# Two graph-attention layers in fp32: work moved at the edges of every stage, fillers for TensorE in two gaps, and the last attention's scaling on GpSimd

## The chip, the core and the metric

The kernel runs on one core of one Trainium2 chip. It uses five engines that run side by side, each with an instruction queue of its own: TensorE (PE in the profile) for matrix products, VectorE (DVE), ScalarE (ACT), GpSimd (POOL) and SyncE (SP), which here only starts transfers. The metric is the time of one execution on the device in microseconds (us); lower is better. Everything is in fp32.

## The reference, cut to what matters

There are N = 4096 nodes with F = 512 features, four heads of D = 128 features, and an adjacency matrix `adj` of 0 and 1. Both layers are residual and normalise their input first:

```python
# layer 0
h   = relu(layernorm(x));  Xw = per head: Xh @ W
s   = sigmoid(f1[:, None] + f2[None, :])          # f1, f2: one number a node and head
att = softmax of adj*s over the neighbours        # both masks are adj, so one attention
Xn  = batchnorm(att @ Xw)                         # the encoder's attention
emb = batchnorm(elu(Xn @ We.T + be) + Xn)         # MLP block
Y   = elu((att @ emb) @ W.T)                      # the decoder's attention, same weights
x   = x + batchnorm(elu(Y @ Wd.T + bd) + Y)       # MLP block
# layer 1
h     = relu(layernorm(x));  feats = h @ W1[head]
logit = leaky_relu(e_s[:, None] + e_n[None, :], 0.2), masked by adj
x     = x + relu(softmax(logit) @ feats + b)      # the last attention ("gat")
```

## The kernel before

**Stages.** The kernel runs through: a front (layer norm of row groups of 512 nodes, transposition, head values and scores), the encoder's attention `enc`, an MLP block, products with W, the decoder's attention `dec`, a second MLP block with residual, layer 1's layer norm and values, and the last attention `gat`. Features mostly lie along the 128 partitions and nodes along the free axis.

**An attention** (`attention()`, L212 to L427) is a loop over 8 blocks (4 heads times 2 halves of TB = 2048 target nodes). Each block has 32 steps j, one per 128 source nodes. A step makes one tile of unnormalised weights `e` of 128x2048. For `enc` and `dec` it is tanh and exp on ScalarE and a product with the mask on VectorE (L435 to L437); for `gat` a relu on ScalarE (L833) and one VectorE instruction that adds a column and multiplies by the mask (L834). TensorE then multiplies the values of the 128 sources with the tile into four PSUM banks of 128x512 (L359; the fourth bank joins at step EVICT = 2, and takes the first two steps then, L356). `weight_tile` (L239 to L244) hands out the buffers for `e`: two come from the pool `keep`, which outlives the MLP blocks, the others from a pool of the attention itself. As `made` is counted up before it is tested, the first tile comes from the own pool and the next ones follow in turn; of each cycle of EP + ebufs tiles, two are from `keep`.

**The softmax's denominators** are sums of the weight tiles over all sources. For each block three lists at L62 to L68 say how a step is summed: "moved" steps are added into a buffer by an accumulating transfer that GpSimd issues (L373), "by ones" steps are summed on TensorE by four matmuls with ones (L252), and all others are added to `acc` on VectorE (L379, L381). At a block's end PE sums the buffers with ones too; with the flag True in `GAT`, the moved buffer's sum follows in the next block's step 1. The decoder reads every fifth weight tile back from memory (`ekeep`, L333) and uses the inverses of the encoder.

**A block's end** is spread over the next block's steps (`ending`, L284 to L301): outputs leave PSUM on ScalarE (`out_gat` L839), denominators are inverted, spread over the partitions by small transfers that GpSimd issues (L277), and each of the four 128x512 outputs is multiplied by its inverse (`scaled_gat`, L843, on VectorE) and goes through a relu with bias (L846) to an accumulating transfer into the output (L852). The last block has no block after it: after its last weight it takes the denominators, then the last step's products (`early` at L363), inverts on VectorE, spreads the inverses by a matmul (L425) and adds the residual on VectorE (L849).

**MLP block and layer 1.** `mlp_block` multiplies 128x512 tiles on PE (L592), takes elu as exp and relu on ScalarE (L612, L613) and two VectorE instructions, and collects the batch norm's statistics. Sixteen small matmuls sum the decoder's MLP weights for its bias (L682), issued where the decoder's attention begins. After the second MLP block, 16 small matmuls build score columns (L726), copied into `w1x` at L728; `residual` (L692 to L706) applies the batch norm and adds x, and `centred` (L733 to L754) takes, for each of eight groups of 512 nodes, the mean by a matmul with 1/F over a sum `S`, three or four differences, relu and squares on ScalarE, and a reduction over the four feature groups (L753). `deviation` (L756) makes the standard deviations, L776 the values and scores of each 128 nodes, L781 their copies. GpSimd sums the values (L787). Then the maximum of the scores is found and broadcast (L796 to L805), exponentials of scores are taken (L807 to L815), and `gat` starts with `row0`, the first row of target scores, which was stored and loaded back (L791 to L793).

**What sets the order.** A scheduler places the instructions of each engine by its own estimates, subject to the data and to edges written by hand: `tc.issue_after(i)` and `pinned([...])` put instructions behind i in their engine's queue. Within a queue the order is then fixed: an instruction that waits holds back all behind it.

Of the kernel before, what the change touches and what calls it, by code (L numbers as in the profile page):

```python
# [31 lines left out]
FP = mybir.dt.float32  # L32
# [8 lines left out]
IB = 512  # L41
# [25 lines left out]
GAT = tuple(range(3, 28, 2)), (30, 31), True  # L67
GAT_LAST = (3, 5, 7, 9, 11, 13, 15, 17, 19, 21, 23), (12, 30, 31)  # L68
# [16 lines left out]
def kernel(ctx, tc, x, xT, adjT, w0, w0T, v0, wencT, wdecT, vecs, w1, w1T, a1, outT):  # L85
# [21 lines left out]
    def bank1():  # L107
        return psum1.tile([P, IB], FP, name="den")

# [102 lines left out]
    def attention(what, keep, pools, weights, values, row_of, out, finish, ebufs, modes=None, invert=None,  # L212
                  kept=None, sums=None, sums2=None, extras={}, row0=None, masks0=()):
# [25 lines left out]
        def weight_tile():  # L239
            nonlocal made  # L240
            made += 1
            if made % (EP + ebufs) < EP:
                return keep.tile([P, TB], FP, name="e", tag="ek", bufs=EP)
            return spool.tile([P, TB], FP, name="e", bufs=ebufs)  # L244
# [66 lines left out]
        for n, (h, tb) in enumerate(blocks):  # L311
# [6 lines left out]
            po, ahead = [bank() for _ in range(SB - 1)], []  # L318
            adds, held, stores, next_row = [], [], [], None
            for j in range(NJ):  # L320
# [4 lines left out]
                with pinned([a_load, *products_of] if j else []):  # L325
                    if (n, j) in extras:
                        extras[n, j](a_load)
                    if not last and j == NJ - 10:
                        next_row = next_row_of(*blocks[n + 1])
# [4 lines left out]
                else:  # L334
# [5 lines left out]
                    products_of = weights(e, rowb, a, j, h, SB if n + j == 0 else 1)  # L340
# [23 lines left out]
                early = last and j == NJ - 1 and invert is not None  # L364
                if not early:
                    products()
# [28 lines left out]
                if early:  # L395
                    products()
# [5 lines left out]
            if not last:  # L402
# [6 lines left out]
                continue  # L409
            outs = [out(spool, h, tb, s, po[s]) for s in range(SB)]  # L410
# [31 lines left out]
    with tc.tile_pool(name="keep", bufs=1) as keep:  # L442

        with tc.tile_pool(name="f_small", bufs=1) as small, tc.tile_pool(name="f_work", bufs=2) as work:
# [26 lines left out]
            for ib in range(NIB):  # L471
                st = work.tile([P, C, 6], FP, name="st")
                mv = work.tile([P, C, 2], FP, name="mv")

                with pinned([first_hn] if ib == 1 else []):
                    for c in range(C):
                        nc.vector.bn_stats(st[:, c, :], xs[ib][:, c, :])
                for c in range(C):
                    nc.vector.bn_aggr(mv[:, c, :], st[:, c, :])
                rstd = work.tile([P, C], FP, name="rstd")  # L480
                last_dve = rsqrt(rstd, mv[:, :, 1], LN_EPS)
                hT = work.tile([P, C, IB], FP, name="hT")
                for c in range(C):
                    by_pool = c == C - 1
# [99 lines left out]
        def mlp_block(work, w, src, dst, gamma, beta, scale, between, early=None):  # L584
# [5 lines left out]
            def product(z, o, ib, lo, hi):  # L590
                for fb in range(lo, hi):
                    nc.tensor.matmul(z, w[:, fb, o * P:(o + 1) * P], nodes(src[fb], ib),  # L592
                                     start=(fb == 0), stop=(fb == C - 1))

            for o in range(C):
# [7 lines left out]
                for ib in range(NIB):  # L603
# [3 lines left out]
                    else:  # L607
                        z = bank()
                        product(z, o, ib, 0, C)
# [12 lines left out]
                last = bn_coefs(stats, gamma, beta, a_mlp, b_mlp, o, o + 1)  # L622
            return last
# [42 lines left out]

        nc.sync.dma_start(w, wdecT.rearrange("(c p) o -> p c o", p=P))
        with tc.tile_pool(name="dec", bufs=1) as spool:
            attention("dec", keep, spool, tanh_weights, xc, lambda h, tb: (rows[tb], h), out_dec, (scaled, elu), 4,
                      kept="read")  # L670
# [5 lines left out]
    with tc.tile_pool(name="l_small", bufs=1) as small, tc.tile_pool(name="l_work", bufs=2) as work:  # L676
        x1 = [R[2]] + [small.tile([P, N], FP, name=f"x1_{o}") for o in range(1, C)]

        pb = bank1()
        for o in range(C):  # L680
            for fb in range(C):
                nc.tensor.matmul(pb[:, o:o + 1], w[:, fb, o * P:(o + 1) * P], ones[:, 0:1],  # L682
                                 start=(fb == 0), stop=(fb == C - 1))
        nc.vector.tensor_sub(bias, vec_of("dec_mlp_b"), pb[:, 0:C])
# [7 lines left out]
        def residual(o, ib):  # L692
# [4 lines left out]
            nc.vector.tensor_add(d, d, xt)  # L697
            if o == 1:
                nc.gpsimd.tensor_add(S[ib], nodes(x1[0], ib), d)
            elif o > 1:  # L700
# [4 lines left out]
            elif ib == NIB - 1:  # L705
                nc.sync.dma_start(outT[o * P:(o + 1) * P, :], x1[o])  # L706

# [7 lines left out]
        last_coefs = mlp_block(work, w, xd, x1, "dec_mlp_bn_gamma", "dec_mlp_bn_beta", None,  # L715
# [6 lines left out]
        pw = bank1()  # L722
        for fb in range(C):
            for h in range(H):
                k = 2 * (fb * H + h)
                nc.tensor.matmul(pw[:, k:k + 2], w1Ts[:, h, fb * P:(fb + 1) * P], a1s[:, h, :], start=True, stop=True)  # L726
        with tc.issue_after(last_coefs.ins):
            nc.vector.tensor_copy(w1x[:, :, :, D:DX], pw[:, 0:2 * C * H].rearrange("p (c h s) -> p c h s", h=H, s=2))  # L728
# [4 lines left out]
        def centred(ib):  # L733
# [3 lines left out]
            residual(C - 1, ib)  # L737
            pm = bank()
            nc.tensor.matmul(pm, mean_of, S[ib], start=True, stop=True)
# [6 lines left out]
            for fb in range(C):  # L746
                if ib:
                    nc.scalar.activation(sq[:, fb, :], d[:, fb, :], AF.Square)
                nc.scalar.activation(hT[:, fb, :], d[:, fb, :], AF.Relu)  # L749
# [3 lines left out]
            nc.vector.tensor_reduce(S[ib], sq.rearrange("p c n -> p n c"), AX.X, ALU.add)  # L753
            return hT  # L754
# [9 lines left out]
        hT = centred(0)  # L764
        rstd = deviation(0)
        for ib in range(NIB):
            for c in range(C):

                if c == 1 and ib < NIB - 1:
                    hT_next = centred(ib + 1)  # L770
                j = ib * C + c
                r = rstd[:, c:c + 1]
                for k in range(2):
                    b = bank()
                    for fb in range(C):
                        nc.tensor.matmul(b[:, 0:2 * DX], hT[:, fb, c * P:(c + 1) * P],  # L776
                                         w1x[:, fb, 2 * k:2 * k + 2, :].rearrange("p h x -> p (h x)"),
                                         start=(fb == 0), stop=(fb == C - 1))
                    pv = heads_of(b)
                    for h in range(2):  # L780
                        nc.scalar.activation(block(v1[2 * k + h], j), pv[:, h, 0:D], AF.Identity, scale=r)  # L781
                    nc.vector.tensor_scalar_mul(scores_of(j, k), pv[:, :, D:DX], r)
# [7 lines left out]
            if ib == SB - 1:  # L790
                store_rows(rows1[0], targets(0))  # L791
                row0 = w.rearrange("p c f -> p (c f)")
                load_row(row0, rows1[0], 0)  # L793
# [4 lines left out]
        nc.tensor.transpose(pt[0:H, 0:P], mloc, ident)  # L798
# [5 lines left out]
        nc.tensor.matmul(pm[:, 0:H], ones[0:H, :], mdiag, start=True, stop=True)  # L804
# [4 lines left out]
        last_act = nc.scalar.activation(jcol, jcol, AF.Exp)  # L809
        nc.vector.tensor_scalar_mul(nq, jcol2, -1.0)  # L810

        for row, in in_parts(SB, row0):
            last_dve = nc.vector.tensor_scalar(row, row, mbc[:, 0:1], G_MAX, ALU.add, ALU.min)
            with tc.issue_after(last_act.ins):
                last_act = nc.scalar.activation(row, row, AF.Exp, scale=0.8)  # L815

    def rest_of_rows(load):

        pss = bank()
        for h in range(H):  # L820
            nc.tensor.matmul(pss[:, h:h + 1], vacc[:, h, :], ones[:, 0:1], start=True, stop=True)
# [9 lines left out]
    def gat_weights(e, rowb, a, j, h, parts):  # L831
        for e, rowb, a in in_parts(parts, e, rowb, a):
            last_act = nc.scalar.activation(e, rowb, AF.Relu, bias=column(nq, j, h), scale=column(jcol, j, h))  # L833
# [8 lines left out]
    def scaled_gat(spool, h, tb, s, o, rb, last):  # L842
        nc.vector.tensor_mul(o, o, rb)  # L843
# [10 lines left out]
    with tc.tile_pool(name="gat", bufs=1) as spool:  # L854
        x1_last = []

        def load_last(load):
# [3 lines left out]
        attention("gat", spool, spool, gat_weights, v1, lambda h, tb: (rowsg, tb * H + h), out_gat,  # L861
                  (scaled_gat, add_to_output), 7, lambda n: (GAT_FIRST, *[GAT] * (H * NTB - 2), GAT_LAST)[n],
# [44 lines left out]
```

## Time and profile before

| what | value |
|---|---|
| time, median of 3 runs (range) | 3273.88 us (3273.81 to 3275.61) |
| span of the profiled execution | 3271.8 us |
| busy PE / DVE / ACT / POOL | 3196.2 / 2675.9 / 2600.1 / 465.7 us |
| products of weights and values, L359 | 2628.8 us over 6048 records |
| gat's weights, L834 (128x2048 form) | 593.0 us, mean 2332 ns |
| gat's additions to the sum, L381 (R<-R,e) | 278.0 us over 121, mean 2298 ns |

The profile's page gives busy time by engine, by line and by a chain that ended last. A group's row names line, engine, operation, output and inputs, count, busy time, the mean of one instruction in ns, and the engine's idle time before them with what ended it. A fp32 matmul shows as two records, and its weight load (PEld) overlaps other matmuls. PE's clock is what the chip granted, 1.0 being full speed; it is read per stretch of time, as busy time alone does not tell a slow matmul from a fast one.

### The profile page before, as it was taken

To read this page: it belongs to the slowest core of one execution; us is meant where nothing else is said; L and a number is where in the kernel's file an instruction comes from. 1 tells how busy PE (TensorE), PEld (TensorE's weight loads), DVE (VectorE), ACT (ScalarE), POOL (GpSimd) and SP (SyncE) were. 2 spreads that over 40 slices of the span, in tenths; PEclk is the share of its full clock that TensorE was granted. 3 is DMA by queue.
4 is the path that set the end of the run, shared out by engine and by line. 5 is a ranking of instruction groups with operands and counts; after the bars stand their busy time and mean duration, and the time that the engine had idled before them with its cause. 6 is when DMAs were issued, how large, how long until landed. Compare 5 with 4: busy or idle time off the path is not lost.

```text
span 3271.8 us, 26021 instructions
## 1 busy us (share of the span) xinstructions
PE 3196.2 (98%) x8719; PEld 1484.0 (45%) x8719; DVE 2675.9 (82%) x1916; ACT 2600.1 (79%) x1901; POOL 465.7 (14%) x622
## 2 busy tenths in 40 slices
PE   7999999999999999999999999999999999999999
PEld 6334434444444464444444444448644444444443
DVE  6999999999999665656665665586599999999997
ACT  7999999999997449999999999565666666665663
POOL 3001211211210000000000000024312222222221
PEclk9999999999999999999999999999999999999999
DMA  9998988988986023444443444232398999889985
GB/s 208 196 195 228 268 222 225 266 222 230 271 234 157 0 68 126 151 130 136 140 151 127 132 148 133 63 132 79 84 213 214 219 228 244 214 204 236 224 217 135
DMA packets 211151, 578.48 MB, mean 177 GB/s; under 512 B 25069, under 2 KB 28173, under 8 KB 195017
## 3 DMA queue, kind: packets, MB, share of 16 engines
q0 software_dynamic: 67968, 222.51, 35.9%
q1 hardware_dynamic: 126432, 293.72, 27.1%
q10 hardware_dynamic: 16616, 60.60, 4.7%
q8 instruction: 68, 1.11, 0.1%
q14 instruction: 67, 0.54, 0.0%
HBM read 377.10 MB, written 84.29 MB: 141 GB/s over the span
## 4 chain that ended last, share of the span: by engine, by line
PE 73%; DVE 10%; ACT 7%; issue 5%; DMA 5%; POOL 0%; DVEq 0%; ACTq 0%; SPq 0%; POOLq 0%
PE ps L359 58%; PE ps L592 7%; DVE e L437 6%; ACT e L435 4%; PE ps L776 3%; DMA a<-mask 3%; ACT e L436 2%; DVE acc L381 2%; DMA acc<-e 2%; PE den L252 1%; PE ps L356 1%; PE ps L648 1%; PE ps L516 1%; DMA rinvs<-dcol 1%; PE ps L498 0%
## 5 line engine op out<-in xcount | busy, mean ns | idle before, releaser
L359 PE MATMUL ps<-e,R 128*128 128x512 f32 x6048 | 2628.8, 595 | 40.3 <-DVE e L437 32.9
L359 PEld LDWEIGHTS ps<-e,R 128*128 128x128 f32 x6048 | 1147.0, 191 | 1512.8 <-issue 1420.0
L437 DVE TENSOR_TENSOR e<-e,a 128x2048 f32<-128x2048 f32 (+1 forms) x470 | 1052.4, 2261 | 381.3 <-ACT e L436 367.1
L435 ACT ACTIVATE e<-rowb,score 128x2048 f32<-128x2048 f32 (+1 forms) x470 | 912.7, 1968 | 102.1 <-PE ps L359 58.1
L436 ACT ACTIVATE e<-e 128x2048 f32<-128x2048 f32 (+1 forms) x470 | 871.0, 1880 | 6.4
L833 ACT ACTIVATE e<-rowb,nq,jcol 128x2048 f32<-128x2048 f32 x224 | 460.8, 2089 | 269.2 <-DMA w<-e 136.6
L834 DVE SCALAR_TENSOR_TENSOR e<-e,jcol,a 128x2048 f32<-128x2048 f32 (+1 forms) x259 | 593.0, 2332 | 10.8 <-ACT e L833 10.8
L381 DVE TENSOR_TENSOR acc<-acc,e 128x2048 f32<-128x2048 f32 x130 | 297.3, 2287 | 2.1
L381 DVE TENSOR_TENSOR R<-R,e 128x2048 f32<-128x2048 f32 x121 | 278.0, 2298 | 0.0
L373 POOL DMA_DIRECT2D w<-e x178 | 150.3, 847 | 609.4 <-DMA w<-e 383.3
L592 PE MATMUL ps<-R,w 128*128 128x512 f32 x512 | 220.3, 592 | 0.6 <-DVE w L550 0.6
L373 POOL DMA_DIRECT2D acc<-e x144 | 120.4, 880 | 540.8 <-DMA acc<-e 222.9
L277 POOL DMA_DIRECT2D rb<-rinvs x60 | 34.2, 574 | 1062.5 <-DVE R L540 871.6
L592 PEld LDWEIGHTS ps<-R,w 128*128 128x128 f32 x512 | 97.2, 190 | 122.7 <-issue 117.4
L776 PE MATMUL ps<-w1x,hT 128*128 128x260 f32 x512 | 118.5, 391 | 1.8 <-ACT hT L749 1.8
L612 ACT ACTIVATE ex<-ps,bias 128x512 f32<-128x512 f32 x64 | 44.0, 687 | 95.9 <-PE ps L592 78.8
L776 PEld LDWEIGHTS ps<-w1x,hT 128*128 128x128 f32 x512 | 98.7, 194 | 21.6 <-ACT hT L749 3.4
L833 ACT ACTIVATE e<-w,nq,jcol 128x2048 f32<-128x2048 f32 (+1 forms) x35 | 65.7, 1938 | 30.8 <-DMA R<-e 30.8
L614 DVE SCALAR_TENSOR_TENSOR ex<-ex,re 128x512 f32<-128x512 f32 x64 | 45.0, 704 | 36.1 <-ACT re L613 35.9
L781 ACT ACTIVATE R<-ps,rstd 128x128 f32<-128x128 f32 x128 | 38.3, 369 | 38.1 <-PE ps L776 37.0
L787 POOL TENSOR_TENSOR vacc<-vacc,R 128x128 f32<-128x128 f32 x120 | 53.0, 468 | 57.5 <-ACT R L781 57.5
L252 PE MATMUL den<-e,ones 128*32 128x512 f32 x440 | 53.0, 598 | 0.0
(162 smaller groups left out, 1228.6 us busy)
## 6 DMA issues: line engine op xcount, KB each, us to landing
a<-mask SPq DMA_DIRECT2D x720, 256.0 KB, 4.3
w<-e POOLq DMA_DIRECT2D x178, 512.0 KB, 6.6
acc<-e POOLq DMA_DIRECT2D x144, 512.0 KB, 7.0
ekeep<-e ACTq DMA_DIRECT2D x48, 1024.0 KB, 7.4
e<-ekeep SPq DMA_DIRECT2D x48, 1024.0 KB, 4.9
mask<-in_adjT POOLq DMA_DIRECT2D x8, 2048.0 KB, 104.5
rowb<-rows SPq DMA_DIRECT2D x16, 1024.0 KB, 8.0
rb<-rinvs POOLq DMA_DIRECT2D x60, 256.0 KB, 4.5
```

Of the source, the lines that this page charges most:

```text
L252: last_ones = nc.tensor.matmul(den[s * 32:(s + 1) * 32, :], ones[:, 0:32], t[:, s * IB:(s + 1) * IB], start=start, stop=stop)
L359: last_main = nc.tensor.matmul(b, block(values[h], j), e[:, s * IB:(s + 1) * IB], start=(j == 0), stop=(j == NJ - 1))
L373: nc.gpsimd.dma_start(into_half, e_half, **({"accum_op": ALU.add} if j > moved[0] else {}))
L381: nc.vector.tensor_add(acc, acc, e)
L435: nc.scalar.activation(e, rowb, AF.Tanh, bias=column(score[:, 1], j, h), scale=0.5)
L436: last_act = nc.scalar.activation(e, e, AF.Exp, scale=0.5)
L437: last_dve = nc.vector.tensor_mul(e, e, a)
L592: nc.tensor.matmul(z, w[:, fb, o * P:(o + 1) * P], nodes(src[fb], ib), start=(fb == 0), stop=(fb == C - 1))
L776: nc.tensor.matmul(b[:, 0:2 * DX], hT[:, fb, c * P:(c + 1) * P], w1x[:, fb, 2 * k:2 * k + 2, :].rearrange("p h x -> p (h x)"), start=(fb = ...
L787: nc.gpsimd.tensor_add(vacc[:, h, :], vacc[:, h, :], block(v1[h], j))
L833: last_act = nc.scalar.activation(e, rowb, AF.Relu, bias=column(nq, j, h), scale=column(jcol, j, h))
L834: last_dve = nc.vector.scalar_tensor_tensor(e, e, column(jcol2, j, h), a, ALU.add, ALU.mult)
```

## The change

It edits the transitions between stages and the last attention:

- *Front:* in the first row group, mean and deviation of the first 128 rows are computed by themselves, ahead of the other three.
- *Decoder's start:* the count in `weight_tile` starts one earlier, so the first two weight tiles of each attention come from `keep` and can be made while the stage before still holds its memory. The 16 sums of MLP weights move into steps 6 and 16 of the decoder's second block. The first eight weights of the decoder are kept in order on ScalarE.
- *Layer 1's start:* fillers (`stay_busy`, matmuls of constants into unused banks) stand among the 16 small matmuls; the first group's mean is taken by two matmuls so that the last feature group needs no addition before it; the copy to `w1x` is put after the first residual; the first two groups of values are multiplied ahead of the first deviation; the reduction becomes two additions.
- *Last attention's start:* fillers between the maximum's transpose, broadcast and four small matmuls; `row0`'s exponentials are taken quarter by quarter among the first weights, of which three steps are made in quarters; `row0` is stored and loaded one group of nodes later.
- *Last attention:* the multiplication by the inverses goes to GpSimd except in the last block; step 30 is summed on VectorE, no longer by ones (in the last block neither 30 nor 31 is); in the last block the products of the last two steps come after the denominators, bank by bank.

The fillers compute nothing that is used: they are there so that PE's clock is not lowered. The purpose of the rest is to have work ready for PE at the edges of the stages, and to take additions off PE and multiplications off VectorE. The core of the diff:

```diff
-GAT = tuple(range(3, 28, 2)), (30, 31), True
-GAT_LAST = (3, 5, 7, 9, 11, 13, 15, 17, 19, 21, 23), (12, 30, 31)
+GAT = tuple(range(3, 28, 2)), (31,), True
+GAT_LAST = (3, 5, 7, 9, 11, 13, 15, 17, 19, 21, 23), (12,)
...
+    def stay_busy(behind, n=1, cols=IB):
+        for _ in range(n):
+            with tc.issue_after(behind.ins):
+                behind = nc.tensor.matmul(bank()[:, 0:cols], ident, w0Ts.rearrange("p h d -> p (h d)")[:, 0:cols],
+                                          start=True, stop=True)
+        return behind
...
-            if made % (EP + ebufs) < EP:
+            if (made - 1) % (EP + ebufs) < EP:
...
-                with pinned([a_load, *products_of] if j else []):
+                with pinned([a_load, *products_of, last_main] if j else []):
...
-                    products_of = weights(e, rowb, a, j, h, SB if n + j == 0 else 1)
+                    with pinned(products_of[:1] if kept == "read" and n == 0 and j < 8 else []):
+                        products_of = weights(e, rowb, a, j, h, SB if NJ * n + j < in_parts0 else 1)
...
-                early = last and j == NJ - 1 and invert is not None
-                if not early:
+                if last and invert is not None and j >= NJ - (1 if kept is not None else 2):
+                    late.append((j, e))
+                else:
                     products()
...
+            for s, b in enumerate(po):
+                for k, t in late:
+                    nc.tensor.matmul(b, block(values[h], k), t[:, s * IB:(s + 1) * IB], start=(k == 0),
+                                     stop=(k == NJ - 1))
...
+                last_dve = deviations(0, 1 if ib == 0 else C)
...
+                    if ib == 0 and c == 1:
+                        last_dve = deviations(1, C)
...
-                      kept="read")
+                      kept="read", extras={(1, 6): sums_of_weights, (1, 16): bias_of_decoder})
...
         for fb in range(C):
-            for h in range(H):
-                k = 2 * (fb * H + h)
-                nc.tensor.matmul(pw[:, k:k + 2], w1Ts[:, h, fb * P:(fb + 1) * P], a1s[:, h, :], start=True, stop=True)
+            with tc.issue_after(last_pe.ins):
+                for h in range(H):
+                    k = 2 * (fb * H + h)
+                    last_pe = nc.tensor.matmul(pw[:, k:k + 2], w1Ts[:, h, fb * P:(fb + 1) * P], a1s[:, h, :],
+                                               start=True, stop=True)
+            last_pe = stay_busy(last_pe)
...
+            if ib == 0:
+                with tc.issue_after(last_pe.ins):
+                    nc.tensor.matmul(pm, mean_of, S[ib], start=True, stop=False)
+                nc.tensor.matmul(pm, mean_of, nodes(x1[C - 1], ib), start=False, stop=True)
+                with tc.issue_after(added.ins):
+                    nc.vector.tensor_copy(w1x[:, :, :, D:DX],
+                                          pw[:, 0:2 * C * H].rearrange("p (c h s) -> p c h s", h=H, s=2))
+            else:
+                nc.tensor.matmul(pm, mean_of, S[ib], start=True, stop=True)
...
-            nc.vector.tensor_reduce(S[ib], sq.rearrange("p c n -> p n c"), AX.X, ALU.add)
+            nc.vector.tensor_add(sq[:, 0:2, :], sq[:, 0:2, :], sq[:, 2:4, :])
+            nc.vector.tensor_add(S[ib], sq[:, 0, :], sq[:, 1, :])
...
+        hT, last_relu = centred(0)
+        ahead = [values(hT, c) for c in range(2)]
+        with tc.issue_after(ahead[-1][1].ins):
+            rstd = deviation(0)
...
+    last_pe = stay_busy(last_pe, 3)
...
     def gat_weights(e, rowb, a, j, h, parts):
+        last_act = last_exp
         for e, rowb, a in in_parts(parts, e, rowb, a):
+            if row_parts:
+                row = row_parts.pop(0)
+                with tc.issue_after(last_act.ins), tc.issue_after(last_scalars.ins):
+                    if len(row_parts) < SB - 1:
+                        held(row)
+                    nc.scalar.activation(row, row, AF.Exp, scale=0.8)
...
     def scaled_gat(spool, h, tb, s, o, rb, last):
-        nc.vector.tensor_mul(o, o, rb)
+        (nc.vector if last else nc.gpsimd).tensor_mul(o, o, rb)
```

## The prediction

> **What bounds the kernel now.** I read the page first (engine shares, the chain that ended last), then busy time by stretches, then the chain and the timeline where stretches show idle time.
>
> ```profile
> PE 3196.2 (98%) x8719; PEld 1484.0 (45%) x8719; DVE 2675.9 (82%) x1916; ACT 2600.1 (79%) x1901; POOL 465.7 (14%) x622
> PE 73%; DVE 10%; ACT 7%; issue 5%; DMA 5%; POOL 0%; DVEq 0%; ACTq 0%; SPq 0%; POOLq 0%
> ```
>
> TensorE works 98% of the span, so only its gaps, its slow stretches and its own work can give anything. The stretches (columns: PE, PEld, DVE, ACT, POOL, clock, DMA share, GB/s):
>
> ```profile
> 2193.00:2205.00 12.00, 6.08 (x36) 4.21 (x34) 9.48 (x20) 9.06 (x14) 0.00 (x0) 0.68 0.27 87
> 2205.00:2212.00 7.00, 6.98 (x17) 5.43 (x18) 6.51 (x7) 3.60 (x7) 0.00 (x0) 0.57 0.44 151
> 2337.00:2345.00 8.00, 1.09 (x6) 0.51 (x4) 4.24 (x13) 6.40 (x12) 0.87 (x3) 0.74 0.51 164
> 2345.00:2352.00 7.00, 7.00 (x17) 3.67 (x18) 5.03 (x9) 7.00 (x6) 1.08 (x2) 0.57 0.62 200
> 2925.49:3039.46 113.97, 113.97 (x290) 49.31 (x289) 110.27 (x55) 71.47 (x42) 25.57 (x30) 1.00 0.92 219
> ```
>
> Each gap (before layer 1's values, before the last attention) is followed by about 7 us at clock 0.57. The last line is one block of the last attention: PE sets its 113.97 us, but VectorE needs 110.27 of it. The chain at the decoder's start:
>
> ```profile
> 1194.79 2.58 PE ps L359 x6
> 1197.37 0.86 PE ps L356 x2
> 1198.22 4.24 PE den L682 x32
> ...
> 1202.57 2.30 DVE e L437
> ...
> 1205.01 5.46 PE ps L359 x6
> 1210.46 1.17 PE ps L356 x2
> 1211.63 3.43 PE ps L359 x8
> ```
>
> Two records are one matmul: a 128x512 one takes 3.43/4 = 0.86 us, and 1.8 after a gap (5.46/3).
>
> **What the Trainium skill says.** "TensorE: Matmul & The Clock Gate", section "Part 1: The HAM clock gate", says an idle window of about 3.4 us halves the clock until PE has been busy about as long; the trace agrees (gaps of 2.5 to 5 us, then 0.57), though here recovery takes up to 7 us. "SBUF — State Buffer", section "Who interferes with whom", says a VectorE instruction with two SBUF inputs contends with a GpSimd one that reads SBUF, and the later one blocks. The timeline shows it:
>
> ```profile
> 2185.78 1.58 POOL L701 TENSOR_TENSOR S<-S,x 128x512 f32<-128x512 f32 x1 [2.01 <-DVE x L697]
> 2186.27 1.64 DVE L617 TENSOR_TENSOR x<-R,ex 128x512 f32<-128x512 f32 x1
> 2189.26 0.69 DVE L617 TENSOR_TENSOR x<-R,ex 128x512 f32<-128x512 f32 x1
> ```
>
> The same addition takes 0.69 us alone and 1.64 beside a GpSimd addition: 0.95 lost. The same section says that tensor_reduce never contends; no run here shows that.
>
> **The change, part by part.**
>
> *Front.* One row group's mean and deviation go first. They need about 1.6 us after the data at 4.07 (0.69 + 0.18, then root and reciprocal), so the first transpose moves from 9.5 to about 6.5; but the fourth group, normalised on GpSimd (2.35 us), starts 0.6 later. The encoder behind is held by ScalarE (tanh and exp take about 3.7 us a step, PE 3.43) and by mask transfers. I take 0, bounds +1 and -1.
>
> *Decoder's start.* j=1's weights come from the pool that outlives the MLP, so they are made before it; the 16 small matmuls (4.24 us) move to block 1. From 1194.6 PE does j=0 and j=1, 8 x 0.86 = 6.9, to 1201.5. j=2: ScalarE from 1194.8, tanh and exp 3.9, VectorE 2.3, ready at 1201.1; j=3 is ready 3.7 later, PE wants it 3.4 later; j=4 is loaded. So j=2 starts at 1201.5, not 1211.5: -10.0. PE never waits in this attention afterwards, so the small matmuls cost 4.2 there. Net -5.8 (-4 to -6.5).
>
> *Layer 1's start.* Now, from the MLP's last product (2193.4) to the last value product (2337.4), 144.0. After: 16 small matmuls 3.6 and four fillers 3.4 end at 2200.5; two mean matmuls end at 2202.2 (the sum over the last feature group is no longer awaited); VectorE's first difference 0.7, ScalarE's first relu 0.6 (it no longer stands behind eight residuals, 5.75 us): first product at 2203.6, warm. The two prepared groups end at 2211.6, deviation 1.0, next mean 0.9, two groups 7.1: 2220.6. The second block's square sums arrive there too. Then six periods of 15.78 (measured steady), 0.15 for a transpose, last deviation and 32 products 15.1: 2330.5. That is -6.8 (-3.5 to -7.5). The reduction (3.77 us) becomes additions of about 1.2 and 0.7; in the steady part this is hidden by PE.
>
> *Last attention's start.* The maximum, shift and exponentials shrink by about 0.7 us; fillers (0.4, 0.4, 2.6) keep PE warm. Twelve quarter steps take ScalarE 0.70 each. PE reaches j=2 14.6 us after the last value product, not 18.5. But VectorE reaches j=4 only 0.9 earlier, since its work is unchanged, and at the first block's end it adds every step (2.26 + 2.20 = 4.47 us a step against 3.43). Now its lead at j=31 is only 0.35 us (weight ready at 2455.36, PE starts it at 2455.7). So only -1.2 survives (-3.5 if VectorE were faster).
>
> *Blocks 1 to 6.* PE loses one ones-step: 0.9, to 113.08. VectorE's demand, from one block's last weight to the next one's while it never waits, is 110.2 (32 x 2.26 + 16 x 2.20 + 4 x 0.60 + 0.25). The added step gives +2.2, the four scalings leave (-2.4): 110.0. But four GpSimd multiplications of 128x512 read SBUF among saturated two-input VectorE work. GpSimd's cost per block is 4 x 1.26 and lies in its waits; VectorE's stall is bounded by 0 and 1.07 each, and I take the 0.96 seen most: 3.8. So 113.85: VectorE sets the pace, 6 x (113.85 - 113.92) = -0.4. Behind a waiting multiplication on GpSimd stand the accumulating transfers (its queue waits 21 us a block for the sum buffer, so there is room), and the relu on ScalarE waits for it (37 us idle a block).
>
> *Tail.* The last block has 19 additions (17 before): VectorE needs 32 x 2.26 + 19 x 2.20 + 0.25 + 3.8 = 118.3 from PE's j=31 of block 6. PE reaches the denominators at 3.4 + 1.8 + 30 x 3.43 + 1.8 = 110.0 and idles 8.3, so it is cold: denominator and eight late products 7.8 + 3.0, then the 9.8 from the broadcasts to the end: 138.9. Before: 3271.8 - 3139.2 = 132.6. So +6.3 (-5 if VectorE kept a lead).
>
> Sum: -5.8 - 6.8 - 1.2 - 0.4 + 6.3 = -7.9, 3273.9 to 3266.0.
>
> **Rivals.** (a) *GpSimd stalls VectorE little.* For: the mask is an 8-bit operand, and no such pair is in the trace. Against: the pair above. Then PE paces: blocks 6 x -0.9 = -5.4, VectorE's lead returns, and the tail is 110.0 + 0.9 + 6.9 + 9.8 = 127.6, -5.0: -24.2, 3250. (b) *The starts give about half* (a late weight or transfer takes a gap's place; the decoder's j=3 has 0.25 us to spare): -6.9 - 0.4 + 6.3 = -1.0, 3273. (c) *Slower:* each of 28 multiplications holds VectorE for its stretched 1.65 us, queued relus and transfers adding to it: 28 x 0.69 = 19 more, 3285. Against it: the room on GpSimd and ScalarE.
>
> **Numbers.** Main case 0.55, (a) 0.22, (b) 0.13, (c) 0.10. The main case has about 3 us either way, its edge being 3267.3 for 0.2%: faster 0.60, same 0.29, slower 0.11. The range takes in (a) and (b): 3249 to 3275.
>
> **What would show it.** Right: the second and third gap without clock below 0.9; j=2 of the decoder about 7 us after its first product; 137 us between MLP and last value product; VectorE without idle time in blocks 1 to 6 and periods near 113.9; additions and weights beside the multiplications stretched to 3.2 us; PE idle some 8 us before the last denominators. Periods of 113.1 with VectorE waiting would mean (a); PE waits at the starts (b); periods over 115 (c).

## The result, and the profile after

The changed kernel takes 3280.55 us (median of 20 runs, 3273.35 to 3287.45) against 3276.04 us (20 runs) for the kernel before: ratio 1.0014, interval 1.0008 to 1.0021. It is slightly slower, by about 4.5 us; 3266 us, faster, had been predicted. Engine shares and the chain that ended last, on the page of the changed kernel:

```profile
PE 3201.0 (98%) x8675; PEld 1482.5 (45%) x8675; DVE 2695.5 (82%) x1911; ACT 2594.5 (79%) x1908; POOL 550.8 (17%) x650
...
PE 51%; DVE 22%; issue 12%; ACT 8%; DMA 5%; POOL 0%; DVEq 0%; ACTq 0%; POOLq 0%
```

Busy shares hardly moved. The chain did: PE's part fell from 73% to 51% and VectorE's rose from 10% to 22%, so in part of the kernel VectorE now sets the end. The next view is busy time by stretches of the changed kernel (PE, PEld, DVE, ACT, POOL, clock, DMA share, GB/s): the start of layer 1, the start of the last attention, one of its blocks, and the wait before the last denominators with the stretch behind it.

```profile
2196.00:2206.00 10.00, 8.56 (x42) 5.34 (x42) 6.43 (x16) 4.09 (x7) 0.00 (x0) 1.00 0.17 52
2206.00:2213.00 7.00, 7.00 (x32) 5.95 (x33) 4.03 (x6) 4.36 (x8) 0.00 (x0) 1.00 0.09 34
...
2336.00:2340.00 4.00, 4.00 (x7) 1.67 (x6) 2.77 (x5) 3.94 (x7) 0.00 (x0) 0.58 0.54 191
2909.91:3024.85 114.94, 113.91 (x284) 48.79 (x280) 114.87 (x52) 68.01 (x40) 36.53 (x34) 1.00 0.94 220
3249.00:3258.00 9.00, 0.43 (x4) 0.00 (x0) 8.97 (x5) 0.00 (x0) 0.00 (x0) 0.78 0.00 0
3258.00:3265.00 7.00, 6.81 (x15) 2.39 (x16) 4.18 (x3) 0.69 (x1) 0.00 (x0) 0.55 0.00 0
```

In the traces the clock is 1.0 or 0.5 and nothing between; 0.57 or 0.73 is a mean over the stretch. Layer 1 starts at full clock now (0.68 and 0.57 before). The last attention's start still has half clock for a while (0.58 in 2336 to 2340). In the block VectorE is busy 114.87 us of 114.94, and PE has idle time, which it had not in this stage before. At the end PE stands still for nearly 9 us and then works at half clock for most of 7.

Where the time went, stage by stage, worked out from the starts of instructions in the traces. The second trace of the old stages is that of experiment 4, which is the kernel before up to the last attention:

| stretch | before (second trace) | after | change | predicted |
|---|---|---|---|---|
| start to the decoder's first product | 1194.6 (1198.0) | 1199.8 | not clear | 0 |
| decoder's attention | 888.9 (886.6) | 886.0 | -1.6 (mean of 9 traces 886.1) | -5.8 |
| MLP's last product to last value product | 143.8 (142.3) | 136.4 | -6.7 | -6.8 |
| last value product to first denominators | 121.6 (121.5) | 120.9 | -0.6 | -1.2 |
| blocks 1 to 6 of the last attention | 683.5 (683.5) | 686.8 | +3.3 | -0.4 |
| last block to the end | 129.4 (129.5) | 139.1 | +9.6 | +6.3 |

The last five rows add to +4.0, which is the measured difference within its interval; the second MLP block, 109.4 us in both, is left out. The first row scatters by itself: over the twelve traces of kernels with changed starts it runs from 1197.3 to 1205.3, so no single trace tells anything of a few us there.

### The profile page after: what moved, and what is told of

It reads as the page before. It is cut to its first block, busy times and chain, and to the rows that moved or that the text cites. A ratio compares the mean times of both kernels' runs of the same rounds, so it can differ in the third digit from the quotient of the medians.

```text
span 3278.9 us, 26053 instructions
## 1 busy us (share of the span) xinstructions
PE 3201.0 (98%) x8675; PEld 1482.5 (45%) x8675; DVE 2695.5 (82%) x1911; ACT 2594.5 (79%) x1908; POOL 550.8 (17%) x650
## 4 chain that ended last, share of the span: by engine, by line
PE 51%; DVE 22%; issue 12%; ACT 8%; DMA 5%; POOL 0%; DVEq 0%; ACTq 0%; POOLq 0%
PE ps L371 37%; PE ps L613 7%; DVE e L452 7%; DVE e L904 6%; DVE R L394 6%; ACT e L450 4%; PE ps L809 3%; DMA a<-mask 3%; DVE acc L394 2%; ACT e L451 2%; DMA acc<-e 2%; PE ps L670 1%; DMA rinvs<-dcol 1%; ACT e L903 1%; PE ps L537 1%
## 5 line engine op out<-in xcount | busy, mean ns | idle before, releaser
L904 DVE SCALAR_TENSOR_TENSOR e<-e,jcol,a 128x2048 f32<-128x2048 f32 (+1 forms) x265 | 620.9, 2378 | 2.8 <-ACT e L903 2.8
L394 DVE TENSOR_TENSOR R<-R,e 128x2048 f32<-128x2048 f32 x129 | 297.2, 2304 | 0.3
L913 POOL TENSOR_TENSOR R<-R,rb 128x512 f32<-128x512 f32 x28 | 80.1, 2865 | 27.0 <-DMA rb<-rinvs 27.0
L846 POOL TENSOR_TENSOR vacc<-vacc,R 128x128 f32<-128x128 f32 x120 | 65.9, 580 | 45.2 <-ACT R L839 44.8
```

What stands on the lines that cost most here:

```text
L394: nc.vector.tensor_add(acc, acc, e)
L846: nc.gpsimd.tensor_add(vacc[:, h, :], vacc[:, h, :], block(v1[h], j))
L904: last_dve = nc.vector.scalar_tensor_tensor(e, e, column(jcol2, j, h), a, ALU.add, ALU.mult)
L913: (nc.vector if last else nc.gpsimd).tensor_mul(o, o, rb)
```

## The experiments

The theories: **A**, each multiplication on GpSimd costs VectorE about 1.2 us and makes it the bound of the last attention; **B**, step 30's addition alone does; **C**, the front or the encoder became slower. **D** came later: the decoder's small matmuls lower PE's clock wherever they stand. Experiments 1 to 3 and 9 are edits of the changed kernel, 4 of the kernel before, the others of experiment 1's kernel; there is no experiment 8.

### 1 to 3: the two edits of the last attention, undone one by one and together

```diff
# 1 and 3
-        (nc.vector if last else nc.gpsimd).tensor_mul(o, o, rb)
+        nc.vector.tensor_mul(o, o, rb)
# 2 and 3
-GAT = tuple(range(3, 28, 2)), (31,), True
-GAT_LAST = (3, 5, 7, 9, 11, 13, 15, 17, 19, 21, 23), (12,)
+GAT = tuple(range(3, 28, 2)), (30, 31), True
+GAT_LAST = (3, 5, 7, 9, 11, 13, 15, 17, 19, 21, 23), (12, 30, 31)
```

> The changed kernel with only the scaling of the last attention put back on VectorE (step 30 stays an addition). Theory A (each multiplication on GpSimd costs VectorE about 1.2 us by stretching the instructions beside it, and VectorE then sets the pace): VectorE's demand falls to 110.2 + 2.2 = 112.4 us a block, under PE's 113.1, so periods of 113.1, VectorE waits again, the tail shrinks by some 7 us; in all about 15 us under the changed kernel, 3265. Theory B (the added addition of step 30 put VectorE on the path, the multiplications cost it no more than its own scalings did): periods stay near 115, 3279 to 3281. Theory C (the encoder became slower by some 5 us for another reason, and the last attention matters little): 3276 or more.

> The changed kernel with the by-ones lists of the last attention put back (30 and 31), the scaling still on GpSimd. Theory A: VectorE's demand 115.0 - 2.2 = 112.8 a block, so PE sets 113.97 with VectorE waiting about 1 us a block; the last block has two additions fewer, tail about 7 us shorter; about 3270. Theory B: VectorE waits about 3.5 us a block, else the same, 3268. Theory C: 3278.

> The changed kernel with both undone: the last attention's blocks as before, the edges as changed. Theory A: what the starts give alone, dec -3, layer 1 -7.4, last attention -0.7: about 11 under the kernel before if the encoder's 5 us in the one trace are scatter (3265), 5 to 6 under if they belong to the change (3270). Theory B: the same. Theory C: 3270 to 3276, with the encoder's end some 5 us later than before in this trace too.

| last attention | scaling on VectorE | scaling on GpSimd |
|---|---|---|
| steps 30 and 31 by ones | experiment 3: 3264.78, 0.9965 (0.9953 to 0.9978) | experiment 2: 3266.51, 0.9974 (0.9964 to 0.9983) |
| step 30 (in the last block also 31) added on VectorE | experiment 1: 3262.42, 0.9954 (0.9940 to 0.9967) | the change: 3280.55, 1.0014 (1.0008 to 1.0021) |

Neither edit alone is slow; together they are. With VectorE scaling, the added step gives PE its 0.9 us a block. With GpSimd scaling it pushes VectorE over PE. Experiment 2's time lies as near to B (3268) as to A (3270), but VectorE's demand in blocks 1 to 3 is 113.1, 113.4 and 111.9 us, as A has it (112.8); B's wait of 3.5 us a block would mean about 110.5. Groups of instructions on VectorE and GpSimd in 2570 to 3140, first of the changed kernel, then of experiment 1 (count | busy, mean ns of one | idle before):

```profile
L904 DVE SCALAR_TENSOR_TENSOR e<-e,jcol,a 128x2048 f32<-128x2048 f32 x159 | 386.6, 2467 | 0.0
L394 DVE TENSOR_TENSOR R<-R,e 128x2048 f32<-128x2048 f32 x80 | 184.5, 2306 | 0.2
...
L913 POOL TENSOR_TENSOR R<-R,rb 128x512 f32<-128x512 f32 x20 | 53.3, 2669 | 17.1 <-DMA rb<-rinvs 17.1
```

```profile
L904 DVE SCALAR_TENSOR_TENSOR e<-e,jcol,a 128x2048 f32<-128x2048 f32 x165 | 380.5, 2340 | 0.0
L394 DVE TENSOR_TENSOR R<-R,e 128x2048 f32<-128x2048 f32 x80 | 182.5, 2281 | 0.0
L913 DVE TENSOR_TENSOR R<-R,rb 128x512 f32<-128x512 f32 x20 | 13.6, 681 | 0.0
```

A multiplication takes 0.68 us on VectorE and 2.67 on GpSimd in this stretch, and the weights beside it grow: over the last attention of the changed kernel, the 35 weights that overlap a GpSimd multiplication take 3.20 us on average and the others 2.34, the 11 such additions 2.57 against 2.28. That is 35 x 0.86 + 11 x 0.30 = 33.4 us over 28 multiplications, 1.2 each. The timeline of the changed kernel shows one:

```profile
2955.59 4.61 DVE L904 SCALAR_TENSOR_TENSOR e<-e,jcol,a 128x2048 f32<-128x2048 f32 x2
...
2958.43 8.39 POOL L913 TENSOR_TENSOR R<-R,rb 128x512 f32<-128x512 f32 x2 [1.52 <-DMA rb<-rinvs]
...
2960.12 2.28 DVE L394 TENSOR_TENSOR R<-R,e 128x2048 f32<-128x2048 f32 x1
...
2962.32 6.65 DVE L904 SCALAR_TENSOR_TENSOR e<-e,jcol,a 128x2048 f32<-128x2048 f32 x2
...
2968.89 2.28 DVE L394 TENSOR_TENSOR R<-R,e 128x2048 f32<-128x2048 f32 x1
```

Two weights take 4.61 us, their usual length, though the first multiplication has begun, and the next two 6.65. Experiment 1's block, again by stretches:

```profile
2908.27:3021.38 113.11, 113.11 (x284) 49.05 (x280) 113.11 (x56) 72.60 (x43) 25.61 (x30) 1.00 0.94 224
```

PE sets the period. VectorE's demand is read from the ends of each block's last weight: 112.4 us from block to block in experiment 1, as worked out, and its lead over PE at step 31 grows from 0.25 to 7.25 us by block 6. In the changed kernel that lead is 0.8 in block 1 and 0.25 in all others, which is to say none, and the weights' own period is 115.2 in blocks 4 to 6. B, whose experiment 1 was 3279 to 3281, is out. Experiment 3 removes these two edits and is 11.5 us faster than before (7 to 15 by its interval). The starts, and 0.9 us in the tail from the products that now come after the denominators, give -9.8. That leaves no room for C's 5 us; a loss of 1 or 2 in the encoder, as in experiment 6, fits too.

### 4: only the multiplications on GpSimd, in the kernel before

```diff
-        nc.vector.tensor_mul(o, o, rb)
+        (nc.vector if last else nc.gpsimd).tensor_mul(o, o, rb)
```

> The kernel before with only the scaling put on GpSimd (in all blocks but the last). Theory A: VectorE instructions beside a multiplication stretched by about 1.2 us in all, demand 110.2 - 2.4 + 4.8 = 112.6 a block, under PE's 113.97: periods unchanged, VectorE's lead grows by 1.4 us a block instead of 3.7, time within 1 us of before. Theory B: no stretching beyond 0.6 us each, lead grows by 3.7 or more a block, time the same. A clear slowdown would mean a stall of more than 1.6 us each.

3275.72 us, ratio 0.9999 (0.9991 to 1.0008). The periods stay at 113.97. VectorE's lead at step 31 of the first three blocks is 0.36, 1.43, 2.66 (0.35, 3.79, 7.56 before), and its demand 112.57, 112.73 and 111.93: A, and a price of (112.4 - 107.8) / 4 = 1.15 us each. Taking the scalings off VectorE costs VectorE more than it saves: 1.15 against 0.60.

### 5: the front

```diff
-                last_dve = deviations(0, 1 if ib == 0 else C)
+                last_dve = deviations(0, C)
...
-                    if ib == 0 and c == 1:
-                        last_dve = deviations(1, C)
```

> Experiment 1's kernel (the change with the scaling on VectorE, 3262.4) with the front put back: all four row groups' deviations first. Theory A (the front hides behind the transfers of x): same time, 3262 +- 2, first transpose at 9.7 again and not 6.5, first tanh within the scatter of 63 to 67. Theory C (the new front and the encoder behind it became slower): 3260 or less and a first tanh near 64.

3261.72 us, 0.9957 (0.9942 to 0.9973): the same as experiment 1. In the changed kernel the first transpose starts at 6.4 instead of 9.5, as worked out, but the first values start at 14.4 in both traces. The gain of 3 us ends there. C finds no support: the first tanh of this trace came at 69.6, later than with the new front (64.6 to 66.9), and later than the 63 to 67 expected.

### 6: the rotation of the weight tiles

```diff
-            if (made - 1) % (EP + ebufs) < EP:
+            if made % (EP + ebufs) < EP:
```

> Experiment 1's kernel with the weight tiles handed out as before (one tile of the own pool first). Theory A: the decoder's second weight can't be made before the MLP ends, PE idles about 4 to 7 us at its start and is at half clock for 7 after it, so some 8 to 10 us are lost: 3271. Theory C (the new rotation also costs the encoder 2.7 us in its second and third block): the encoder falls back to 249 us for these two blocks and the loss is 6: 3268. Rival (the other edits of that start, the moved sums, give the gain): under 3265.

In the kernel before it is the second tile, not the first, that comes from the attention's own pool: `made` is 1 when it is first tested, and EP is 2.

3259.99 us, 0.9954 (0.9938 to 0.9971): no loss, against the expectation of A of 8 to 10 us, and in the range of the rival. Two causes show. PE does idle at the decoder's start, but for 3.02 us only and at full clock behind it, for the small matmuls no longer stand there; the decoder takes 888.2 us against 886.0. And the encoder gains: its second block, from one first tanh to the next, takes 126.5 to 127.3 us in the four traces where the encoder has the old rotation and 128.0 to 128.8 in the ten with the new one. So the new rotation spares 1.7 us of waiting in the decoder (3.02 against 1.32) and takes 1.5 in the encoder.

### 7: the fillers

```diff
-        for _ in range(n):
+        for _ in range(0):
```

> Experiment 1's kernel without the filler matmuls (they compute nothing that is used). Theory A: the products after the second MLP block start at the same time, as the chain through VectorE and ScalarE sets it, but at half clock for about 7 us: +3.5; the last attention's start cold as well, +1 to +3.5 of which little survives: 3266. Rival (fillers useless, the clock stays up without them): 3262. Rival (fillers delay the work behind them): 3259.

3262.14 us, 0.9961 (0.9946 to 0.9976), not to be told from experiment 1 by its time. By stages it is clear: MLP to last value product 138.7 us instead of 136.4, at a lowered clock:

```profile
2195.00:2205.00 10.00, 6.45 (x35) 4.05 (x34) 6.40 (x16) 4.05 (x6) 0.00 (x0) 0.73 0.15 52
2205.00:2212.00 7.00, 6.82 (x21) 5.56 (x22) 4.29 (x7) 4.58 (x9) 0.00 (x0) 0.65 0.05 19
```

and last value product to first denominators 120.9 in both. The fillers of layer 1 are worth 2.3 us. Those of the last attention are worth nothing: of the eleven traces with fillers, five have 3.4 us of half clock at its start and six have none, and the stretch takes 120.9 us in all. PE's clock does not set it.

### 9: every multiplication on GpSimd twice

```diff
...
+        if not last:
+            nc.gpsimd.tensor_mul(spare, o, rb)
         (nc.vector if last else nc.gpsimd).tensor_mul(o, o, rb)
```

> The changed kernel with each GpSimd multiplication of the last attention preceded by a second one into a spare tile that nothing uses (56 instead of 28). Theory A (each costs VectorE 1.2 us, and VectorE sets the pace): periods of 115.1 + 4 x 1.2 = 119.9, the tail 4.8 longer, 3280.5 + 6 x 4.8 + 4.8 = 3314. Theory B (the multiplications cost VectorE no more than 0.3 us each): 3280 to 3288.

3309.36 us, 1.0102 (1.0087 to 1.0117). The weights' periods in blocks 4 to 6 are 120.35, 119.63 and 120.31, mean 120.1: 4.9 over the changed kernel's 115.2 for four more multiplications, 1.23 each. The whole is 5 us under the 3314 expected, since the early periods are shorter (117 to 118). A holds with a dose, not only with a switch.

### 10: the decoder's small matmuls, spread

The 16 one-column matmuls of L694 of the changed kernel go into steps 6, 8, 10 and 12, four at a time.

```diff
...
-                      kept="read", extras={(1, 6): sums_of_weights, (1, 16): bias_of_decoder})
+                      kept="read", extras={**{(1, 6 + 2 * o): lambda load, o=o: sums_of_weights(o) for o in range(C)},
+                                           (1, 16): bias_of_decoder})
```

> Experiment 1's kernel with the 16 one-column matmuls of the decoder's weight sums put in four groups of four (steps 6, 8, 10, 12 of the decoder's second block) and not all at step 6. Theory D (3.6 us of one-column matmuls count as idle for the clock, which falls to half speed for some 4 us after them, wherever they stand): no stretch of clock under 0.9 near 1330 to 1345, and the decoder takes 884.3 us from its first product to the MLP's, against 884.3 to 887.6 (mean 886.2) in the seven traces with all 16 together. Rival (the clock falls by chance, or by the throttle, at that point): the same mean and scatter as before.

3257.31 us, 0.9943 (0.9929 to 0.9957): by its whole time not told from experiment 1, but by the decoder's. The stretches around the small matmuls, first of the changed kernel (all 16 at 1332), then of this one:

```profile
1330.00:1334.00 4.00, 4.00 (x25) 2.81 (x23) 2.46 (x2) 3.97 (x3) 0.00 (x0) 1.00 0.44 150
1334.00:1338.00 4.00, 4.00 (x19) 2.57 (x19) 2.46 (x2) 2.57 (x2) 0.00 (x0) 0.73 0.24 66
1338.00:1342.00 4.00, 4.00 (x10) 1.69 (x9) 0.93 (x1) 1.10 (x1) 0.00 (x0) 0.85 0.29 68
```

```profile
1328.00:1332.00 4.00, 4.00 (x17) 2.28 (x16) 2.46 (x2) 3.97 (x3) 0.00 (x0) 1.00 0.30 115
1332.00:1336.00 4.00, 4.00 (x11) 1.84 (x10) 2.45 (x2) 3.97 (x3) 0.00 (x0) 1.00 0.22 66
1336.00:1340.00 4.00, 4.00 (x16) 2.22 (x15) 2.43 (x2) 3.97 (x3) 0.00 (x0) 1.00 0.25 66
```

PE counts as busy throughout in both, yet the clock falls in the first. The decoder takes 884.25 us here, and 884.25 again in experiment 12, where they are spread too; with all 16 together it took 884.25 to 887.6 in nine traces, seven of them over 885.9.

Chance as the rival for this scatter can be settled from the traces. The Trainium skill ("TensorE: Matmul & The Clock Gate", "Part 1: The HAM clock gate") says that activity is judged over windows that run freely, and the traces agree: in each of the 14, all changes of the clock lie a whole number of 3.41 us apart. Here are the small matmuls alone by such windows (PE, PEld, clock, DMA share, GB/s), first of the changed kernel, then of experiment 3, whose clock did not fall:

```profile
1332.42:1335.83 3.41, 3.20 (x29) 3.11 (x28) 1.00 0.19 71
1335.83:1339.25 3.42, 0.00 (x0) 0.00 (x0) 0.50 0.28 77
```

```profile
1329.92:1333.34 3.42, 1.75 (x17) 1.94 (x17) 1.00 0.41 130
1333.34:1336.75 3.41, 1.88 (x17) 1.79 (x17) 1.00 0.30 68
```

Of the ten traces with all 16 together the clock falls in eight, each time after a window with 2.70 to 3.33 us of small matmuls. In the other two (experiments 3 and 9) the edge between two windows cuts them in halves of 1.75 to 1.88 us; spread, at most 0.95 us lie in one window. The same split holds over the whole of the 14 traces, counting by window the time in which PE had matmuls of more than four columns: full clock turned to half after 73 windows, which had at most 1.65 us of it, and stayed full after 13109, which had at least 1.39; half clock turned to full only after windows with 2.76 us or more. So D stands, with one correction to "wherever they stand": the fall depends on where the window's edge lies. Of the three falls in the kernel before that the prediction deals with, those at 1200.7 and 2197.4 end windows in which small matmuls kept PE busy for 2.66 and 3.03 us; only that at 2340.8 follows mere idle time.

### 11: a GpSimd instruction of one input

The scaling is on VectorE; each output has one more GpSimd instruction, whose result nothing uses.

```diff
...
+        if not last:
+            nc.gpsimd.tensor_scalar_mul(spare, rb, 2.0)
         nc.vector.tensor_mul(o, o, rb)
```

> Experiment 1's kernel (scaling on VectorE) with one more GpSimd instruction of one SBUF input for each output: the inverses times 2 into a spare tile that nothing uses, 28 in all. Theory A as the skill words it (a GpSimd instruction that reads SBUF and a two-input VectorE one shut each other out): VectorE instructions beside it stretched by about 1.2 us each, demand 112.4 + 4.8 = 117.2 a block, some 3295 to 3300. Rival (only a GpSimd instruction of two inputs takes what VectorE needs): no stretching, demand 112.4, 3262.

3295.27 us, 1.0059 (1.0045 to 1.0073): the time that A gave, and yet not its mechanism. GpSimd's row, and timeline lines of both engines (columns of the row: shortest, median, longest in ns):

```profile
L914 POOL TENSOR_SCALAR spare<-rb x28: 1489/2547/33457, 2502.0 to 3233.9; 128x512 f32<-128x512 f32 x28
```

```profile
2501.98 36.61 POOL L914 TENSOR_SCALAR spare<-rb 128x512 f32<-128x512 f32 x3 [1.88 <-DMA rb<-rinvs]
...
2517.67 6.87 DVE L904 SCALAR_TENSOR_TENSOR e<-e,jcol,a 128x2048 f32<-128x2048 f32 x3
...
2538.53 1.81 POOL L386 DMA_DIRECT2D w<-e  x2
...
2545.72 2.09 ACT L903 ACTIVATE e<-rowb,nq,jcol 128x2048 f32<-128x2048 f32 x1 [31.42 <-DMA w<-e]
...
2550.51 25.09 PE L371 MATMUL ps<-e,R 128*128 128x512 f32 x51 [9.19 <-DVE e L904]
```

The first of the 28 is shut out. It takes 33.5 us where the shortest takes 1.49, while VectorE goes on at its usual pace beside it (three weights in 6.87 us), and it ends 1.4 us after VectorE has run out of work at 2534.08. Behind it stand the accumulating transfers, so weight tiles don't come free. ScalarE, which in this attention also issues the small transfers of the inverses (not GpSimd), waits 31 us, and PE 9. The first two periods are 127.1 and 124.5 us; in them PE is idle for 15 us and at half clock for 20. Blocks 4 to 6 are at 113.1 again, and the tail is 8 us longer.

The other 27 take 1.5 to 6.2 us and do stretch VectorE, but less than a multiplication does: the 40 weights beside such an instruction take 2.51 us instead of 2.34, the 21 additions 2.42 instead of 2.28, ten scalings 0.89 instead of 0.68. Together that is 12.0 us, 0.43 for each of the 28, against 1.2. Both expectations fall: the one that named a stretching of 1.2 us, and the one that took a single input for harmless.

### 12: spread sums, and the old rotation in the encoder alone

```diff
# on experiment 10's kernel
-            if (made - 1) % (EP + ebufs) < EP:
+            if (made - (kept != "write")) % (EP + ebufs) < EP:
```

> Experiment 10's kernel with the encoder's weight tiles handed out as before and the new rotation only in the decoder and after. If the new rotation costs the encoder 2.5 us in its second and third block (126.9 + 122.4 with the old one against 128.4 + 123.5), and the spread sums save 1.9 on average: 3262.4 - 4.4 = 3258. If neither does: 3262.

3258.72 us, 0.9944 (0.9931 to 0.9958). The encoder's second block is back at 126.7 us, but its third took 124.6 in this trace (it scatters from 121.1 to 125.0 in all), and the time isn't told from experiment 10's. Experiments 10 and 12 have the lowest ratios, some 18 us or 0.56% under the kernel before, but their intervals overlap with experiment 1's.

### 13: no values ahead of the first deviation

```diff
-        ahead = [values(hT, c) for c in range(2)]
-        with tc.issue_after(ahead[-1][1].ins):
-            rstd = deviation(0)
+        ahead = []
+        rstd = deviation(0)
```

> Experiment 1's kernel without the two groups of values multiplied ahead of the first deviation. Theory A (the first deviation, about 1 us of small matmuls behind ScalarE's squares and VectorE's two additions, holds PE up): PE waits some 4 us for squares, additions and deviation while nothing else is ready, and the stretch from the MLP's last product to the last value product takes 139 to 141 us, not 136.4; 3265. Rival (the fillers and the two mean matmuls give the whole gain): 136.4, 3262.

3262.20 us, 0.9952 (0.9939 to 0.9966); the stretch takes 136.4 us, as with the edit. PE's order tells why the run decides little: without the edit the scheduler puts the deviation behind 14 of the 16 value products of the two groups by itself. The edit writes down nearly what happens anyway.

## Why the prediction was wrong

It gave -7.9 us and +4.0 was found in the stages; nearly all of the difference of 12 lies in three terms. In the decoder a step failed: that PE never waits there, and that its small matmuls cost nothing but their own time (4.2 us). In blocks 1 to 6 and in the tail the mechanism was right and two sizes were wrong: a GpSimd multiplication was taken to cost VectorE 0.96 us and costs 1.2, and an addition that VectorE still owed to the tail was left out (2.2 us).

- *Decoder's start, -5.8, found -1.6.* The main step was right: the third weight's products start 6.9 us after the first (17.0 before). What failed is "PE never waits in this attention afterwards, so the small matmuls cost 4.2 there". They take 3.6 us and bring down the clock where they now stand, 1.9 us on average (886.1 - 884.25). PE also waits once, 1.32 us at 1224. ScalarE needs 3.7 to 3.9 us a weight there against PE's 3.43 a step, which the prediction had and followed only as far as j = 3. Another 1.2 us is the base: the trace that the prediction was read from had 10.2 us of half clock at this start, the second trace of the same stage 3.4, and the change is counted from their mean (887.75, not 888.9). That only idle time makes PE cold was half of it: matmuls of one column lower the clock as well.
- *Encoder, held unchanged.* The rotation was costed for the decoder only. It costs the encoder's second block 1.5 us (experiment 6). The first row of the table is too scattered to show the sum.
- *Layer 1's start, -6.8, found -6.7.* Its clock, its first product 10.2 us after the MLP's last and its end are as predicted. Of it 2.3 us are the fillers'; the other 4.4 (the mean by two matmuls, the order of the copy, the additions) were not separated.
- *Last attention's start, -1.2, found -0.6:* right in kind, since the stretch takes the same time whatever PE's clock. That this gap would show no clock below 0.9 was wrong: half clock for 3.4 us from 2335.9, in spite of the fillers.
- *Blocks 1 to 6, -0.4, found +3.3.* The mechanism was right: two-input instructions stretched, VectorE sets the pace. The size was off: 0.96 us taken for a multiplication, 1.15 to 1.23 measured (experiments 4 and 9, and the overlaps in the changed kernel). That makes 4.1 to 5.3 us a block and not 3.8, and periods of 114.1 to 115.3, not 113.85, once the first blocks' small lead is used up. The bound of 1.07 came from pairs in which one short instruction was hit. In the changed kernel most multiplications stay near it and stretch one instruction by 1.0 to 1.1 us, but four of the 28 stretch a weight by 1.7 to 2.0.
- *Tail, +6.3, found +9.6.* PE idles 8.76 us (8.3 predicted) and then takes 11.1 us for the cold denominators and late products (10.8 predicted). The missing 3.5 us come earlier: VectorE needs 121.8 us, not 118.3, from PE's step 31 of block 6 to its last addition. The dearer multiplications are 1 of it. Step 30's addition of block 6 is 2.2: it stands behind weight 31 and was still to be done when the prediction's count began. The last 0.3 is not explained.

VectorE's last lines ahead of the end of the changed kernel, and PE's:

```profile
3251.27 2.33 DVE L904 SCALAR_TENSOR_TENSOR e<-e,jcol,a 128x2048 f32<-128x2048 f32 x1
3253.53 4.60 DVE L394 TENSOR_TENSOR R<-R,e 128x2048 f32<-128x2048 f32 x2
...
3258.19 1.94 PE L262 MATMUL den<-R,ones 128*32 128x512 f32 x8 [8.76 <-DVE R L394]
```

Rival (a) gave 3250 for a small stall. It didn't come true in the changed kernel, but experiment 1 shows its periods of 113.1 and VectorE's lead once the multiplications are back on VectorE. Rival (b) (starts half, 3273) had the right size for the decoder alone. Rival (c) named the direction, by 0.69 us more a multiplication; about 0.25 was found, and the rest came from the tail's addition and the decoder.

## What to carry to other kernels

Moving an elementwise operation off a nearly saturated VectorE onto GpSimd can cost VectorE more than doing it there: compare the stretch of the neighbours (here 1.2 us) with the operation itself (0.6), not the two engines' busy shares. When two edits draw on the same slack (here 3.7 us of VectorE a block), cost them together: each alone was free or a small gain, both were a loss. And an instruction that keeps TensorE busy by the profile may still not keep its clock: look at the clock after stretches of tiny matmuls, and spread them.

## What the runs showed that had not been expected

- Sixteen matmuls of one column, 3.6 us during which PE counts as busy, halve its clock for 3.4 or 6.8 us in eight of ten traces, whenever 2.7 us or more of them fall into one window of 3.41 us. In four groups of four they don't, in both traces.
- A GpSimd multiplication of two SBUF inputs and VectorE's two-input stream slow each other: 2.67 us for 1.26 (GpSimd's addition of the same size at 2147 in the kernel before), and 1.2 us of stretch. A GpSimd instruction of one SBUF input stretched VectorE by 0.43 us on average, and was itself held off once for 33.5 us.
- The Trainium skill ("SBUF — State Buffer", "Who interferes with whom") says that whoever issues first holds the shared ports and the other blocks. The traces agree that one blocks the other, but the first does not always win: in those 33.5 us, 16 VectorE instructions that started after the GpSimd one went before it. Why this happened to one of 28, and to none of the multiplications (5.2 us at most in the changed kernel), is open.
